# First attention of a two-layer gated cross-attention kernel: the last chunk's scores, the weighted sum of two steps back and the next step's first scores as one stretch of TensorE work

## The chip, the cores and the metric

The kernel runs on one core of a Trainium2 chip. The time is the device time of one execution in microseconds (us). The kernel before takes 2732.07 us, the median of three runs (2730.35, 2732.07, 2735.17).

## The reference, cut

Two layers follow each other. Each adds a gated cross-attention of 16 x 100 tokens of width 512 to a context of 16 x 722 rows of width 384, and then a gated feed-forward (in the first layer a mixture of 8 experts, in the second a quantized network). Everything is float32. The change touches the attention, above all that of layer 0:

```python
# layer 0: H = 16 heads, D = 32; layer 1: H = 8, D = 64, no biases on q, k, v
q = (layernorm(x) @ Wq + bq).reshape(B, Nq, H, D).transpose(0, 2, 1, 3)   # B=16, Nq=100
k = (ctx @ Wk + bk).reshape(B, Nkv, H, D).transpose(0, 2, 1, 3)           # Nkv=722
v = (ctx @ Wv + bv).reshape(B, Nkv, H, D).transpose(0, 2, 1, 3)
attn = softmax(clip(einsum('bhqd,bhkd->bhqk', q, k) * D**-0.5, -1e4, 1e4), axis=-1)
x = x + tanh(g_xattn[0]) * (einsum('bhqk,bhkd->bqhd', attn, v).reshape(B, Nq, C) @ Wo + bo)
```

## The kernel before, in words

The program runs layer 0's attention, the routing and the experts, layer 1's attention and the quantized network one after the other. Both attentions are objects of one class, `Attention`. A group holds G heads that fill 128 rows: G is 4 in the first attention (32 rows each) and 2 in the second (64 rows each). One **step** is a pair (b, m), batch b and group m; there are 16 x 4 = 64 steps in each attention.

In a step the keys lie on the 128 partitions, in NS = 6 chunks of the 722 context rows; the last chunk has SL = 82 rows. NS1 is 5. Queries (T = 100) and heads lie along the free dimension. The parts of a step are:

- `scores(b, m, 0)`, L362: the *first scores*, chunks 0 to 4. Twenty matmuls (L372), four heads at a time in 32-row tiles of the array, write one PSUM tile `ps_s`. In the first attention this tile takes four of the eight PSUM banks, and the pool has one buffer of it (`4 // self.G`, L261); in the second it has two. ScalarE copies the tile to the SBUF tile `raw` (L386). VectorE then takes maxima in two reductions (L389): over chunks 0 to 2, and over that result with chunks 3 and 4, into a tile `mx`.
- `scores(b, m, 1)`: the *last chunk's scores*, four matmuls into the same PSUM tile, a copy by ScalarE (L382) and one maximum into `mx` (L384).
- `peaks`, L393: TensorE transposes `mx` (L399), VectorE reduces the transposed maxima over the partitions (L405).
- `softmax`, L407: TensorE transposes the tops back and spreads them over 128 partitions (L413, `ps_top`). VectorE subtracts them from the scores in three instructions (L421: chunks 0 to 2, chunks 3 and 4, the last chunk), ScalarE takes two exponentials of 1200 elements a partition (L427), and GpSimd (VectorE in the second attention) adds the six chunks into `sm` (L430).
- `attend`, L435: the *weighted sum*. 24 matmuls (L442) in 32-column tiles form probabilities times values, four more (L453) the denominators from `sm`; VectorE divides (L461, L462).

Besides these there is full-size TensorE work, which I call *dense units*: `keys` (L216, three matmuls of 361 columns), `values` (L241, three of 512), `queries` (L345), `project` (L468), transposes of inputs (L139), and, for the experts that follow, normalized rows and their logits (L657). A float32 matmul that is not a transpose stands as two records in the trace, so a value chunk shows as six.

`run`, L496, writes out the order of TensorE's work. For each step it collects dense units with due times (`first`, `last`) and an even share of their cost. Then it issues, in this order: `peaks` of step i, first scores of step i+1, dense units of a cost of at least 2000 columns, `softmax` of step i, last chunk's scores of step i+1, weighted sum of step i-1, and the rest of the dense units. TensorE keeps that order (`manual_schedule(engines={PE})`). On the other engines a scheduler places the instructions, and each engine runs its own in that order. The dense units, `ps_mx`, `ps_top` and the weighted sum share a PSUM pool `ps_m` of four one-bank buffers.

SP's queue issues the context loads (`load_ctx`, two buffers); a batch's load is issued in the third step of the batch two before it.

Of the kernel before, what the change touches and what calls it, by code (L numbers as in the profile page):

```python
# [8 lines left out]
F32 = mybir.dt.float32  # L9
I32 = mybir.dt.int32  # L10
AF = mybir.ActivationFunctionType
ALU = mybir.AluOpType
AX = mybir.AxisListType
# [3 lines left out]
P = 128  # L17
B, T, C = 16, 100, 512
# [5 lines left out]
KC = C // P  # L24
KK = CK // P
NS = -(-S // P)
SL = S - (NS - 1) * P
NS1 = NS - 1
# [12 lines left out]
BIG = 3.0e38  # L41
# [9 lines left out]
def bcast(ap, *shape):  # L51
    return ap.to_broadcast(list(shape))
# [90 lines left out]
class Attention:  # L143
# [113 lines left out]
    def open(self, ctx):  # L257
        tc, nc, name, w = self.net.tc, self.net.nc, self.name, self.w
        pool = lambda n, k, **kw: open_pool(ctx, tc, f"{name}_{n}", k, **kw)
        self.pb, self.pw, self.p2 = pool("b", 1), pool("w", 1), pool("2", 2)  # L260
        self.ps_s, self.ps_m = pool("s", 4 // self.G, space=PSUM), pool("m", 4, space=PSUM)  # L261
        if not hasattr(self, "wq"):
            self.wq = self.pw.tile([P, KC, C], F32, name=f"wq_{name}")
        self.wo = self.pw.tile([P, KC, C], F32, name=f"wo_{name}")
        for n in ("bq", "bv"):
            if n + "_cols" in w:
                self.cols[n] = self.pw.tile([P, KC], F32, name=f"{n}c_{name}")
                nc.gpsimd.dma_start(self.cols[n], w[n + "_cols"])
        self.gbo = self.pw.tile([P, C], F32, name=f"gbo_{name}")

        self.tT = self.pw.tile([P, KC, N], F32, name=f"tT_{name}")

        self.raw = [
            self.pw.tile([P, self.G, NS + 1, T], F32, name=f"raw{i}_{name}") for i in range(2)
        ]
        for t in self.raw:
            nc.gpsimd.memset(t[:, :, NS, :], -BIG)
        self.qT, self.mx, self.top, self.pT = {}, {}, {}, {}

    def load_query_weights(self, pin=False):  # L280

# [80 lines left out]
    def scores(self, b, m, part):  # L362


        nc, D, G = self.net.nc, self.D, self.G
        g, i = divmod(b, GB)
        q = slice(i * T, (i + 1) * T)
        ps = self.ps_s.tile([P, G, 512], F32, tag="s", name="ps_s")
        r = SL if part else P
        for n, c in enumerate((NS - 1,) if part else range(NS - 1)):  # L370
            for j in range(G):
                nc.tensor.matmul(  # L372
                    ps[:r, j, n * T : (n + 1) * T],
                    self.kT[b, m][j * D : (j + 1) * D, c * P : c * P + r],
                    self.qT[g][j * D : (j + 1) * D, m, q],
                    start=True,
                    stop=True,
                )

        st = self.raw[(b * KC + m) % 2]  # L380
        if part:
            nc.scalar.copy(st[:SL, :, NS, :], ps[:SL, :, :T])  # L382
            mx = self.mx[b, m]
            nc.vector.tensor_tensor(mx, mx, st[:, :, NS, :], ALU.max)  # L384
            return
        nc.scalar.copy(st[:, :, :NS1, :].rearrange("p g c t -> p g (c t)"), ps[:, :, : NS1 * T])  # L386
        mx = self.mx[b, m] = self.p2.tile([P, G, T], F32, tag="mx", name="mx", bufs=1)
        for c, to in ((0, st[:, :, NS1, :]), (3, mx)):
            nc.vector.tensor_reduce(  # L389
                to, st[:, :, c : c + 3, :].rearrange("p g c t -> p g t c"), AX.X, ALU.max  # L390
            )

    def peaks(self, b, m):  # L393

        nc, G = self.net.nc, self.G
        mx = self.mx.pop((b, m))
        ps = self.ps_m.tile([T, G, P], F32, tag="mm", name="ps_mx")
        for j in range(G):
            nc.tensor.transpose(ps[:, j, :], mx[:, j, :], self.net.ident)  # L399
        if self.extremes is None:  # L400
            self.top[b, m] = self.p2.tile([T, G], F32, tag="top", name="top")
        else:
            h = b * self.heads + m * G
            self.top[b, m] = self.extremes[:, h : h + G]
        nc.vector.tensor_reduce(self.top[b, m], ps, AX.X, ALU.max)  # L405

    def softmax(self, b, m):  # L407

        nc, G = self.net.nc, self.G
        top, st = self.top.pop((b, m)), self.raw[(b * KC + m) % 2]  # L410
        ps = self.ps_m.tile([P, G, T], F32, tag="mm", name="ps_top")
        for j in range(G):
            nc.tensor.transpose(ps[:, j, :], bcast(top[:, j : j + 1], T, P), self.net.ident[:T, :T])  # L413
        t = self.p2.tile([P, 2, G, 3, T], F32, tag="pT", name="pT")

        late = b == B - 1 and m
        adds = nc.gpsimd if G == 4 else nc.vector
        sm = None if late else self.p2.tile([P, G, T], F32, tag="sm", name="sm")
        for part in range(2):
            for c, z, at in ((0, 3, 0),) if part == 0 else ((0, 2, 3), (2, 3, NS)):  # L420
                nc.vector.tensor_tensor(  # L421
                    t[:, part, :, c:z, :],
                    st[:, :, at : at + z - c, :],
                    bcast(ps.unsqueeze(2), P, G, z - c, T),
                    ALU.subtract,
                )
            nc.scalar.activation(t[:, part], t[:, part], AF.Exp)  # L427
            for n in () if late else range(3):
                if part or n:
                    adds.tensor_tensor(  # L430
                        sm, t[:, part, :, n, :], sm if part or n > 1 else t[:, 0, :, 0, :], ALU.add
                    )
        self.pT[b, m] = t, sm

    def attend(self, b, m):  # L435
        nc, D, G = self.net.nc, self.D, self.G
        t, sm = self.pT.pop((b, m))
        ps = self.ps_m.tile([P, 2, T], F32, tag="mm", name="ps_pv")
        for c in range(NS):
            n = P if c < NS - 1 else SL  # L440
            for j in range(G):
                nc.tensor.matmul(  # L442
                    ps[j * D : (j + 1) * D, 0, :],
                    self.v[b][:n, c, m * P + j * D : m * P + (j + 1) * D],
                    t[:n, c // 3, j, c % 3, :],
                    start=(c == 0),
                    stop=(c == NS - 1),
                )

        parts = [sm] if sm is not None else [t[:, c // 3, :, c % 3, :] for c in range(NS)]  # L450
        for k, of in enumerate(parts):
            for j in range(G):
                nc.tensor.matmul(  # L453
                    ps[j * D : (j + 1) * D, 1, :],
                    self.net.ones[:, :D],
                    of[:, j, :],
                    start=(k == 0),
                    stop=(k == len(parts) - 1),
                )
        rs = self.p2.tile([P, T], F32, tag="rs", name="rs")  # L460
        nc.vector.reciprocal(rs, ps[:, 1, :])  # L461
        nc.vector.tensor_tensor(self.tT[:, m, b * T : (b + 1) * T], ps[:, 0, :], rs, ALU.mult)  # L462
# [33 lines left out]
    def run(self, done=(), after_project=None, more=()):  # L496
# [14 lines left out]
        for b in range(B):  # L511
            for i in tiles_for(b):

                at = (b + 1) * KC + (1 if b != B - 2 else KC - 1)
                extra[at].append((self.project, i))
                for later, *unit in after_project(i) if after_project else ():
                    extra[at + later].append(tuple(unit))
        todo = [u for b in range(1, B) for u in self.keys_and_values(b) if u not in done]

        def do(units):  # L520
            for f, *a in units:
                f(*a)

        def first(unit):

            f, b, n = unit[:3]
            return 4 * (b - 1) + n - 1 if f == self.keys else 4 * (b - 1) if b > 1 else -1

        def last(unit):

            f, b, n = unit[:3]
            return 4 * b + n - 2 if f == self.keys else 4 * b

        end = len(steps) - 2
        for i in range(-1, len(steps)):
# [11 lines left out]
                    todo.remove(unit)  # L547
                    spent += self.cost(unit)

            units.sort(key=lambda u: u[0] in (self.keys, self.values) and first(u) == i)  # L550
            nxt = steps[i + 1] if i + 1 < len(steps) else None
            u = self.cut(units, 2000)
            if i >= 0:
                self.peaks(b, m)
            if nxt:
                self.scores(*nxt, 0)
            if self.G == 4:
                do(u[0])
                if i >= 0:
                    self.softmax(b, m)  # L560
            if nxt:
                self.scores(*nxt, 1)
            if i > 0:
                self.attend(*steps[i - 1])
            if self.G == 2:
                do(u[0])
                if i >= 0:
                    self.softmax(b, m)
            do(u[1])
        self.attend(*steps[-1])  # L570
        for i in range(len(steps), len(steps) + 40):
            do(extra[i])
# [1045 lines left out]
```

## Time and profile before

| what | value |
|---|---|
| median of three runs | 2732.07 us |
| the profiled execution, its own time | 2731.8 us |
| its span, first to last instruction | 2730.1 us |
| granted TensorE clock, mean over the span | 0.992 |
| first attention, first scores of step 1 to those of step 63 | 55.3 to 864.26 us |
| TensorE busy in that stretch | 799.5 of 809.0 us |
| VectorE, ScalarE, GpSimd busy in that stretch | 546.3, 415.0, 357.0 us |

The profile names an engine PE (TensorE's matmuls), PEld (its weight loads), DVE (VectorE), ACT (ScalarE), POOL (GpSimd) or SP. A row of the time line gives the start in the span, the busy time and the group of instructions; what stands in brackets is how long the engine was idle before and which instruction ended that. `L372 PE MATMUL ps_s<-qT_a,kT_a 32*128` is a matmul of line 372 with 32 rows and 128 columns of weights. The trace also has each instruction's own record, from which the spacings of matmuls are read. Matmul ends are modelled, so it is the starts that count.

### The profile page before, as it was taken

The page shows a single profiled execution, that of the slowest core. Times are in us where ns is not written, and L with a number is a line of the kernel's source. Part 1 is how long each engine was busy: PE and PEld are TensorE (multiplying, and loading weights), DVE is VectorE, ACT ScalarE, POOL GpSimd, SP SyncE. Part 2 cuts the span into 40 slices and gives each one's busy share as a digit, 9 for nine tenths or more (in the row PEclk, how much of TensorE's full clock was granted, in tenths as well). Part 3 has the DMA queues.
Part 4 walks back from the last instruction along what each step waited for, and adds up shares of the span by engine and source line. Part 5 has one row for each costly group of instructions (what it writes and reads, how often), then busy time and mean ns, then how long its engine had stood idle before and what let it go on. Part 6 is the DMA issues. An engine that isn't in the chain of part 4 may idle for free. (4 is left out here: it accounts for less than half of the span.)

```text
span 2730.1 us, 45777 instructions
## 1 busy us (share of the span) xinstructions
PE 2682.5 (98%) x19716; PEld 1740.7 (64%) x19716; DVE 1201.2 (44%) x2010; ACT 859.0 (31%) x1194; POOL 499.3 (18%) x497
## 2 busy tenths in 40 slices
PE   8999999999998999999999999999999999899999
PEld 5666666666565688888888766666666566445554
DVE  4666676666667301010101077666565555611100
ACT  2545554545454100000000046333333333311110
POOL 2534444444442000000000042000000000301000
PEclk9999999999999899999999999999999999999999
DMA  5001000010001499989899432000000010610000
GB/s 167 18 18 34 18 29 22 18 45 18 18 29 57 169 360 348 320 313 321 310 318 319 166 91 63 21 22 29 17 23 27 17 34 1 185 62 16 12 12 10
DMA packets 129190, 278.33 MB, mean 102 GB/s; under 512 B 5825, under 2 KB 5841, under 8 KB 128465
## 3 DMA queue, kind: packets, MB, share of 16 engines
q1 hardware_dynamic: 117888, 246.80, 26.2%
q0 software_dynamic: 5968, 19.17, 2.1%
q10 hardware_dynamic: 5120, 9.31, 0.9%
q8 instruction: 160, 2.62, 0.4%
q14 instruction: 54, 0.43, 0.0%
HBM read 260.31 MB, written 14.94 MB: 101 GB/s over the span
## 5 line engine op out<-in xcount | busy, mean ns | idle before, releaser
L241 PE MATMUL ps_v<-wv_a,ctx_a 128*128 128x512 f32 (+1 forms) x1152 | 520.2, 599 | 1.0 <-DVE pT L421 0.5
L216 PE MATMUL ps_k<-ctx_a,wk_a 128*128 128x361 f32 x1488 | 485.5, 473 | 3.2 <-DVE pT L421 2.1
L874 PE MATMUL ps_h<-xT,w 128*128 128x128 f32 x3712 | 422.1, 276 | 4.0 <-DVEq L1503 4.0
L874 PEld LDWEIGHTS ps_h<-xT,w 128*128 128x128 f32 x3712 | 419.5, 193 | 4.7 <-issue 4.7
L216 PEld LDWEIGHTS ps_k<-ctx_a,wk_a 128*128 128x128 f32 x1488 | 272.6, 190 | 164.0 <-issue 18.3
L241 PEld LDWEIGHTS ps_v<-wv_a,ctx_a 128*128 128x128 f32 (+1 forms) x1152 | 204.8, 184 | 243.1 <-issue 229.9
L427 ACT ACTIVATE pT<-pT 128x1200 f32<-128x1200 f32 (+1 forms) x256 | 243.2, 953 | 258.2 <-DVE pT L421 248.0
L421 DVE TENSOR_TENSOR pT<-raw_a,ps_top 128x400 f32<-128x400 f32 (+4 forms) x384 | 279.0, 771 | 11.2 <-PE ps_top L413 11.0
L430 POOL TENSOR_TENSOR sm<-pT,sm 128x400 f32<-128x400 f32 x244 | 252.5, 1035 | 38.4 <-ACT pT L427 21.7
L389 DVE TENSOR_REDUCE raw_a<-raw_a 128x400 f32<-128x1200 f32 (+1 forms) x128 | 152.1, 1188 | 218.0 <-ACT raw_a L386 217.9
L386 ACT COPY raw_a<-ps_s 128x2000 f32<-128x2000 f32 (+1 forms) x128 | 180.3, 1408 | 154.1 <-PE ps_s L372 153.7
L372 PE MATMUL ps_s<-qT_a,kT_a 32*128 32x100 f32 (+3 forms) x4608 | 214.2, 277 | 3.4 <-ACT raw_a L386 1.2
L885 DVE TENSOR_TENSOR midT<-silu,ps_h 128x512 f32<-128x512 f32 x58 | 39.9, 688 | 390.4 <-PE ps_h L874 390.4
L894 PE MATMUL ps_o<-w,midT 128*128 128x512 f32 x464 | 203.9, 592 | 0.0
L372 PEld LDWEIGHTS ps_s<-qT_a,kT_a 32*128 32x128 f32 (+3 forms) x4608 | 180.1, 180 | 35.8 <-issue 22.7
L1100 PE MATMUL ps_z<-ffn_w,y_ffn 128*128 128x512 f32 (+1 forms) x416 | 190.8, 594 | 0.0
L248 ACT COPY v_a<-ps_v 128x512 f32<-128x512 f32 x192 | 111.3, 581 | 248.3 <-PE ps_v L241 248.3
L1082 PE MATMUL ps_y<-hT,ffn_w 128*128 128x384 f32 (+2 forms) x512 | 183.6, 503 | 0.0
L442 PE MATMUL ps_pv<-pT,v_a 128*32 128x100 f32 (+3 forms) x4608 | 163.2, 254 | 7.3 <-ACT pT L427 7.3
L442 PEld LDWEIGHTS ps_pv<-pT,v_a 128*32 128x32 f32 (+3 forms) x4608 | 135.5, 120 | 22.6 <-ACT pT L427 8.7
L1082 PEld LDWEIGHTS ps_y<-hT,ffn_w 128*128 128x128 f32 x512 | 95.1, 190 | 84.6 <-issue 50.3
L894 PEld LDWEIGHTS ps_o<-w,midT 128*128 128x128 f32 x464 | 85.9, 190 | 97.1 <-issue 97.1
(169 smaller groups left out, 2211.3 us busy)
## 6 DMA issues: line engine op xcount, KB each, us to landing
w<-in_L_ffn_w SPq DMA_DIRECT2D x116, 1024.0 KB
w<-in_L_ffn_wo SPq DMA_DIRECT2D x29, 2048.0 KB
ctx_a<-in_ctxT SPq DMA_DIRECT2D x30, 1083.0 KB
q<-in_L_ffn_fc_q SPq DMA_DIRECT2D x8, 1024.0 KB
ffn_w<-in_L_ffn_fc_scales SPq DMA_DIRECT2D x8, 1024.0 KB
rows<-ot ACTq DMA_DIRECT2D x29, 256.0 KB
xn_d<-xn_moe POOLq DMA_DIRECT2D x11, 256.0 KB, 2.3
ctx_a<-in_ctxT SPq DMA_DIRECT2D x6, 361.0 KB
```

The lines of the kernel that those rows point to most:

```text
L216: nc.tensor.matmul(ps, self.wk[:, k, m * P : (m + 1) * P], self.cxs[b][:, k, c * SH : (c + 1) * SH], start=(k == 0), stop=(k == KK - 1),)
L241: nc.tensor.matmul(ps[:n], self.cxs[b][:, k, c * P : c * P + n], self.wv[:, k, :], start=(k == 0), stop=(k == KK - 1),)
L372: nc.tensor.matmul(ps[:r, j, n * T : (n + 1) * T], self.kT[b, m][j * D : (j + 1) * D, c * P : c * P + r], self.qT[g][j * D : (j + 1) * D, ...
L386: nc.scalar.copy(st[:, :, :NS1, :].rearrange("p g c t -> p g (c t)"), ps[:, :, : NS1 * T])
L421: nc.vector.tensor_tensor(t[:, part, :, c:z, :], st[:, :, at : at + z - c, :], bcast(ps.unsqueeze(2), P, G, z - c, T), ALU.subtract,)
L427: nc.scalar.activation(t[:, part], t[:, part], AF.Exp)
L430: adds.tensor_tensor(sm, t[:, part, :, n, :], sm if part or n > 1 else t[:, 0, :, 0, :], ALU.add)
L442: nc.tensor.matmul(ps[j * D : (j + 1) * D, 0, :], self.v[b][:n, c, m * P + j * D : m * P + (j + 1) * D], t[:n, c // 3, j, c % 3, :], start ...
L874: nc.tensor.matmul(ph[:, f, :], w[:, n, k, f * P : (f + 1) * P], self.xT[j][:, k, :], start=(k == 0), stop=(k == KC - 1),)
L894: nc.tensor.matmul(po, self.midT[j, f // 4][:, f % 4, :], w[:, f, :], start=(f == 0), stop=(f == KF - 1),)
L1082: nc.tensor.matmul(ps[:, :nt], w1[f // nf][:, k, f % nf * P : (f % nf + 1) * P], hT[g][:, k, :nt], start=(k == 0), stop=(k == KC - 1),)
L1100: nc.tensor.matmul(z[j][:n], y[:, j * P : j * P + n], w2[f // nf][:, f % nf, :], start=(f == 0), stop=(f == NF - 1),)
```

## The change

Seven edits, all in `Attention`:

1. In the first attention (G = 4) `run` issues, for step i: last chunk's scores of step i, weighted sum of step **i-2**, first scores of step i+1, dense units of at least 2500 columns, `peaks` of step i, dense units of at least 1500, `softmax` of step i, and the rest. At the end the weighted sums of the last two steps remain.
2. In the second attention the order of the calls stays as it was.
3. The due times of keys, values and projections move by one step in the first attention.
4. The tile `mx` goes. `raw` has seven chunks; now the last chunk's scores lie in place 5 and the maxima in place 6, behind them. Place 5 holds the maximum of chunks 0 to 2 until the last chunk's scores overwrite it.
5. The last chunk is treated on its 82 rows only (maximum, subtraction, exponential, addition, denominator), so the two memsets of `raw` go.
6. The softmax has three exponentials (1200, 800 and 400 elements in the first attention) in place of two of 1200, each behind its own subtraction, in both attentions.
7. Line numbers shift: in the changed kernel the matmuls of the scores are L370, the last chunk's copy L380, the maximum L382, the first scores' copy L384, the reductions L386, the subtractions L422, the exponentials L425, the additions L427, the weighted sum L439 and L451.

```diff
-        for t in self.raw:
-            nc.gpsimd.memset(t[:, :, NS, :], -BIG)
...
         if part:
-            nc.scalar.copy(st[:SL, :, NS, :], ps[:SL, :, :T])
-            mx = self.mx[b, m]
-            nc.vector.tensor_tensor(mx, mx, st[:, :, NS, :], ALU.max)
+            nc.scalar.copy(st[:SL, :, NS1, :], ps[:SL, :, :T])
+            mx = st[:SL, :, NS, :]
+            nc.vector.tensor_tensor(mx, mx, st[:SL, :, NS1, :], ALU.max)
             return
...
-        mx = self.mx[b, m] = self.p2.tile([P, G, T], F32, tag="mx", name="mx", bufs=1)
-        for c, to in ((0, st[:, :, NS1, :]), (3, mx)):
+        for c, to in ((0, NS1), (3, NS)):
...
-        for part in range(2):
-            for c, z, at in ((0, 3, 0),) if part == 0 else ((0, 2, 3), (2, 3, NS)):
-                nc.vector.tensor_tensor(
-                    t[:, part, :, c:z, :],
-                    st[:, :, at : at + z - c, :],
-                    bcast(ps.unsqueeze(2), P, G, z - c, T),
-                    ALU.subtract,
-                )
-            nc.scalar.activation(t[:, part], t[:, part], AF.Exp)
...
+        for a, z in ((0, 3), (3, NS - 1), (NS - 1, NS)):
+            r = P if z < NS else SL
+            to = t[:r, a // 3, :, a % 3 : a % 3 + z - a, :]
+            nc.vector.tensor_tensor(
+                to, st[:r, :, a:z, :], bcast(ps[:r].unsqueeze(2), r, G, z - a, T), ALU.subtract
+            )
+            nc.scalar.activation(to, to, AF.Exp)
...
-                at = (b + 1) * KC + (1 if b != B - 2 else KC - 1)
+                at = (b + 1) * KC + (KC - 1 if b == B - 2 else 2 if self.G == 4 else 1)
...
-            return 4 * (b - 1) + n - 1 if f == self.keys else 4 * (b - 1) if b > 1 else -1
+            lag = self.G == 4
+            at = 4 * (b - 1) + n - 1 if f == self.keys else 4 * (b - 1) if b > 1 else -2
+            return at + lag
...
-            return 4 * b + n - 2 if f == self.keys else 4 * b
+            return 4 * b + n - 2 if f == self.keys else 4 * b + (self.G == 4)
...
+            if self.G == 4:
+
+                if i >= 0:
+                    self.scores(b, m, 1)
+                if i > 1:
+                    self.attend(*steps[i - 2])
+                if nxt:
+                    self.scores(*nxt, 0)
+                one, units = self.cut(units, 2500)
+                do(one)
+                if i >= 0:
+                    self.peaks(b, m)
+                two, units = self.cut(units, 1500)
+                do(two)
+                if i >= 0:
+                    self.softmax(b, m)
+                do(units)
+                continue
...
-            if self.G == 4:
-                do(u[0])
-                if i >= 0:
-                    self.softmax(b, m)
-            if nxt:
                 self.scores(*nxt, 1)
             if i > 0:
                 self.attend(*steps[i - 1])
...
+        if self.G == 4:
+            self.attend(*steps[-2])
         self.attend(*steps[-1])
```

More of the change, by code (lines that the diff above doesn't have):

```diff
@@ L275, in open @@
         ]
-        for t in self.raw:
-            nc.gpsimd.memset(t[:, :, NS, :], -BIG)
-        self.qT, self.mx, self.top, self.pT = {}, {}, {}, {}
+        self.qT, self.top, self.pT = {}, {}, {}
     def load_query_weights(self, pin=False):
@@ L381, in scores @@
         if part:
-            nc.scalar.copy(st[:SL, :, NS, :], ps[:SL, :, :T])
-            mx = self.mx[b, m]
-            nc.vector.tensor_tensor(mx, mx, st[:, :, NS, :], ALU.max)
+            nc.scalar.copy(st[:SL, :, NS1, :], ps[:SL, :, :T])
+            mx = st[:SL, :, NS, :]
+            nc.vector.tensor_tensor(mx, mx, st[:SL, :, NS1, :], ALU.max)
             return
         nc.scalar.copy(st[:, :, :NS1, :].rearrange("p g c t -> p g (c t)"), ps[:, :, : NS1 * T])
-        mx = self.mx[b, m] = self.p2.tile([P, G, T], F32, tag="mx", name="mx", bufs=1)
-        for c, to in ((0, st[:, :, NS1, :]), (3, mx)):
+        for c, to in ((0, NS1), (3, NS)):
             nc.vector.tensor_reduce(
-                to, st[:, :, c : c + 3, :].rearrange("p g c t -> p g t c"), AX.X, ALU.max
+                st[:, :, to, :],
+                st[:, :, c : c + 3, :].rearrange("p g c t -> p g t c"),
+                AX.X,
+                ALU.max,
             )
@@ L395, in peaks @@
         nc, G = self.net.nc, self.G
-        mx = self.mx.pop((b, m))
+        mx = self.raw[(b * KC + m) % 2][:, :, NS, :]
         ps = self.ps_m.tile([T, G, P], F32, tag="mm", name="ps_mx")
@@ L418, in softmax @@
         sm = None if late else self.p2.tile([P, G, T], F32, tag="sm", name="sm")
-        for part in range(2):
-            for c, z, at in ((0, 3, 0),) if part == 0 else ((0, 2, 3), (2, 3, NS)):
-                nc.vector.tensor_tensor(
-                    t[:, part, :, c:z, :],
-                    st[:, :, at : at + z - c, :],
-                    bcast(ps.unsqueeze(2), P, G, z - c, T),
-                    ALU.subtract,
-                )
[L427 to L431, printed above, removed]
-                    )
+        for a, z in ((0, 3), (3, NS - 1), (NS - 1, NS)):
[5 more added lines that the diff above has]
+            nc.scalar.activation(to, to, AF.Exp)
+            for c in () if late else range(max(a, 1), z):
+                adds.tensor_tensor(
+                    sm[:r], t[:r, c // 3, :, c % 3, :], sm[:r] if c > 1 else t[:, 0, :, 0, :], ALU.add
+                )
         self.pT[b, m] = t, sm
@@ L451, in attend @@
         for k, of in enumerate(parts):
+            n = P if k < NS - 1 else SL
             for j in range(G):
@@ L454, in attend @@
                     ps[j * D : (j + 1) * D, 1, :],
-                    self.net.ones[:, :D],
-                    of[:, j, :],
+                    self.net.ones[:n, :D],
+                    of[:n, j, :],
                     start=(k == 0),
@@ L548, in run @@
                     spent += self.cost(unit)
-            units.sort(key=lambda u: u[0] in (self.keys, self.values) and first(u) == i)
+            if self.G == 2:
+                units.sort(key=lambda u: u[0] in (self.keys, self.values) and first(u) == i)
             nxt = steps[i + 1] if i + 1 < len(steps) else None
-            u = self.cut(units, 2000)
+            if self.G == 4:
[15 more added lines that the diff above has]
+                continue
+            one, units = self.cut(units, 2000)
             if i >= 0:
@@ L564, in run @@
                 self.attend(*steps[i - 1])
[L565 to L569, printed above, removed]
+            do(one)
+            if i >= 0:
+                self.softmax(b, m)
+            do(units)
+        if self.G == 4:
+            self.attend(*steps[-2])
         self.attend(*steps[-1])
```

## The prediction

> **What bounds the kernel now.** I read the page's busy times first, then TensorE's waits inside the first attention, then the time line of one of its steps, and last the two places where the same resource was short.
>
> The page: TensorE is busy for almost the whole span, the other engines are not.
> ```profile
> PE 2682.5 (98%) x19716; PEld 1740.7 (64%) x19716; DVE 1201.2 (44%) x2010; ACT 859.0 (31%) x1194; POOL 499.3 (18%) x497
> ```
> TensorE's waits between the first scores of step 1 (55.3 us) and of step 63 (864.26 us), 62 steps of 13.05 us (9.4 us in all by the idle time ahead of the groups):
> ```profile
> PE ps_mx L399 <- DVE mx L384: 3.4, 2, 2.1
> PE ps_k L216 <- DVE pT L421: 2.1, 2, 1.9
> PE ps_y L468 <- DVE pT L421: 1.9, 1, 1.9
> PE ps_mx L399 <- ACT pT L427: 1.2, 1, 1.2
> PE ps_v L241 <- DVE pT L421: 0.5, 2, 0.3
> ```
> The columns are total, times and longest. Nothing else stops TensorE there, so shorter TensorE work is worth its whole length, and a new wait costs its whole length.
>
> One step on the time line (start, busy us, engine, group):
> ```profile
> 300.92 0.51 PE L413 MATMUL ps_top<-ident,extremes 100*128 100x100 f32 x4
> 301.36 0.41 PE L372 MATMUL ps_s<-qT_a,kT_a 32*82 32x100 f32 x8
> 301.71 1.24 PE L442 MATMUL ps_pv<-pT,v_a 128*32 128x100 f32 x48
> 301.90 0.49 ACT L382 COPY raw_a<-ps_s 82x400 f32<-82x400 f32 x1 [0.19 <-PE ps_s L372]
> 302.77 0.36 PE L453 MATMUL ps_pv<-sm,ones 128*32 128x100 f32 x8
> 302.94 2.77 DVE L421 TENSOR_TENSOR pT<-raw_a,ps_top 128x1200 f32<-128x1200 f32 x3
> 303.05 5.42 PE L241 MATMUL ps_v<-wv_a,ctx_a 128*128 128x512 f32 x12
> 304.42 2.52 ACT L427 ACTIVATE pT<-pT 128x1200 f32<-128x1200 f32 x2 [2.03 <-DVE pT L421]
> 308.31 0.60 PE L399 MATMUL ps_mx<-ident,mx 128*100 128x128 f32 x4
> 308.84 1.37 PE L372 MATMUL ps_s<-qT_a,kT_a 32*128 32x100 f32 x40
> 310.14 0.66 PE L139 MATMUL ps_tr<-ident,xn_a 128*128 128x128 f32 x4
> 310.33 1.83 ACT L386 COPY raw_a<-ps_s 128x2000 f32<-128x2000 f32 x1 [1.24 <-PE ps_s L372]
> ```
> Two things are to be seen. The small-tile work (32-row and 32-column tiles) stands in two places. And ScalarE copies the last chunk's scores (301.90) ahead of the exponentials (304.42), over six microseconds before the next scores (308.84) need their PSUM tile.
>
> **The gain: one change of tile shape fewer.** Single records of the trace give the price. Before 308.84 the spacing is 0.202 us where two transposes stand 0.109 apart: 0.093 lost. After the weighted sum the first full-size matmul starts 0.177 later, and the second 0.533 instead of 0.429 after it: 0.281. The change removes both and adds one boundary, weighted sum to first scores, which no record shows. Bounds are 0.07 (groups inside the weighted sum) and 0.202. I take 0.177, since that spacing was the same before every kind of matmul. Saved: 0.093 + 0.281 - 0.177 = 0.197 us a step, 62 steps: **-12.2 us** (bounds -10.7 and -18.8). The boundary into the last chunk's scores costs 0.09 over the usual spacing before and after the change.
>
> **The new wait on ScalarE.** All scores of this attention go through one PSUM tile (four banks, one buffer). The next step's first scores now come 1.69 us (301.36 to 302.88, + 0.177) after the last chunk's, and must wait until ScalarE has copied those. In the changed program's instruction order ScalarE has, in nearly every step: copy of first scores, copies of the dense units before the top transposes, three exponentials, copies of the units after them, and only then the last chunk's copy. So exponentials that delayed nobody now stand ahead of a copy that TensorE waits for; behind that copy stand the next copy of scores and everything that follows it.
>
> Take a step whose three blocks of dense work are one value chunk each, time 0 at its first scores. TensorE: dense work at 1.303 (308.84 to 310.14), + 0.104 first matmul, value 2.58 (6 x 0.429), maxima's transposes 0.44, value 2.58: top transposes at 7.00. Then 0.35, value 2.58, 0.09, and 1.69 more: next first scores wanted at 11.71. The other chain: subtraction 0.62 after the top transposes begin (445.66 to 446.27): 7.62; exponential 1.48 later (302.94 to 304.42): 9.10; 1.21 for 1200 elements; then 800 and 400 elements, which this trace lacks. The rows of 1200 (1.203) and of 600 in the second attention (0.703) make a line with 0.20 fixed: 0.87 and 0.53. End 11.71; value copy 0.58; last chunk's copy 0.49; 0.06 to TensorE: 12.84. **Wait 1.13 us.** The same sum over all 62 steps, each with its own units in the changed order: 21 steps with one value behind the top, 1.13 each, 23.7; 22 with two key blocks, 0.61 to 0.90, 14.2; 3 with one key block, 1.9 each, 5.7; one with nothing, 3.8; the other 15, where more stands there, 1.6. Together **+49.0 us**. Bounds for the two shorter exponentials: 0.49 (copy of 400) + 0.70, and 0.70 + 1.20: -0.2 and +0.5 a step, -10 and +25 us on some 50 steps.
>
> **The wait at the top transposes.** VectorE's reduction of the transposed maxima (0.69) now stands behind the first, often behind both, reductions of the next step's scores (1.54 each), which begin at 1.49 + 1.83 + 0.04 = 3.36. With a query block ahead of the maxima and one key block behind: 3.36 + 1.54 + 0.62 (query) + 1.54 + 0.69 + 0.10 = 7.86, and TensorE comes at 6.36: 1.50. Such steps: 4 at 1.50, 9 at 0.86 (projection), 5 at 0.74, three more with 2.3 in all; 41 at nothing. **+19.7 us**; bounds 0 (were the reduction ahead) and 25.
>
> **What else goes and comes.** The old waits go, since their causes (maximum late behind the subtractions, a PSUM buffer held by them) now end before the row does: -9.4. Kept maxima: the maximum works on 82 partitions of the same 400 elements, 0.56, and the buffer it no longer shares was never waited for; the two memsets on GpSimd lie in the opening. GpSimd's five additions a step (1.03 each) have one step more to finish. The third exponential adds 0.20 to every step of the second attention, behind TensorE except in its few waits there: +0.5. Opening, one activation table load that falls into the chain, and the last step, where the projection moves ahead of the last maxima (877.69 - 874.45 = 3.2 us at most): 0.8 + 1.6 - 2.5. DMA issues on SP and GpSimd keep their steps; values may fall one step later, and the context load they free, 4.5 us long by the DMA share (issued 319.3, over by 323.8), still has a step of 13 us.
>
> **The clock.** A wait can cost more than itself:
> ```profile
> 595.95:599.37 3.42, 1.49 (x8) 0.94 (x7) 3.42 (x6) 2.36 (x2) 1.20 (x1) 1.00 0.00 0
> 599.37:602.78 3.41, 3.41 (x7) 1.88 (x6) 0.86 (x3) 0.61 (x2) 3.17 (x4) 0.50 0.02 5
> 836.50:840.00 3.50, 2.22 (x20) 1.00 (x22) 3.47 (x6) 1.96 (x3) 2.74 (x3) 1.00 0.00 0
> 840.00:843.40 3.40, 3.40 (x45) 2.05 (x39) 0.94 (x2) 1.82 (x1) 2.31 (x3) 1.00 0.02 5
> ```
> In the first column after the stretch's length TensorE is busy: 1.49 of 3.42 us was followed by a granted clock of 0.50 for 3.41 us, 2.22 of 3.50 was not. Half speed for 3.41 us loses 1.7. Four new waits of about 1.9 us or more, at rather better than half odds: +4 (bounds 0, and 1.7 for each of the 25 of 1.1 or more: 43).
>
> The Trainium skill, "TensorE: Matmul & The Clock Gate", section "Why this matters for your kernels", says that idle gaps up to about 3 us do not throttle. The trace differs: a gap of 1.9 us did. By the page this term would be 0 and the time 4 us less; the rows decide.
>
> **Sum**, against the profiled execution's own 2731.8 us (span 2730.1; 0.3 under the median 2732.07, nothing at this scale): -12.2 + 49.0 + 19.7 - 9.4 + 0.5 - 0.1 + 4 = +51.5, **2783 us**.
>
> **Rivals.** *Faster*: the last chunk's copy is never late. The row is then pure gain: -12.2 - 9.4 and the ends -2, with 0 to 19.7 for the reduction: 2708 to 2728. For it speaks that ScalarE is busy 31% only; against it the fixed order of its instructions, and that it happened in the one place where the tile is refilled at once:
> ```profile
> 865.76 1.82 ACT L386 COPY raw_a<-ps_s 128x2000 f32<-128x2000 f32 x1 [1.37 <-PE ps_s L372]
> 867.64 0.64 PE L372 MATMUL ps_s<-qT_a,kT_a 32*82 32x100 f32 x8 [1.15 <-ACT raw_a L386]
> ```
> It decides where both waits together stay under about 0.35 us a step (22 us). *Clock*: waits of 1.1 us also drop it: +43 in place of +4, 2822. *No gain from the row*: the new boundary costs as much as both old ones: +12, 2795, inside the range.
>
> **Chances.** Forecast 0.70, no gain from the row 0.05, clock 0.09, faster 0.12, waits and gain cancelling 0.04. The range reaches from 2783 - 10 (exponentials) - 7 (boundary) - 16 (most of the reduction's wait) to 2783 + 25 + 10: 2750 to 2818, which leaves out the faster rival and most of the clock's. This kernel's measurement tells 0.2% from no change: faster 0.13, same 0.03, slower 0.84.
>
> **What would show it.** TensorE's first scores (L370) waiting for the last chunk's copy (L380), about 49 us in some 50 waits; top transposes waiting for the reduction L405, about 20 us in 21; spacing 0.18 from weighted sum to first scores. It is wrong if the first scores follow the weighted sum without a wait, or if the exponentials are seen behind the last chunk's copy.

## The result and the profile after

| | before | after |
|---|---|---|
| median of the runs shown | 2732.07 us | **2748.11 us** (four runs, 2745.17 to 2751.44) |
| profiled execution, its own time | 2731.8 us | 2751.44 us |
| its span | 2730.1 us | 2749.4 us |
| first attention, first scores of step 1 to those of step 63 | 808.9 us | 821.6 us |

The ratio is 1.0058 with a 95% interval of 1.004 to 1.0075: the change costs 0.6%. The forecast was slower, 2783, with a range from 2750 to 2818. The direction was right; the size (+51.5 forecast, +16.0 measured) was three times too large, and the range missed the time by 2 us. The profiled execution of the changed kernel is the slowest of its four, 3.3 us above their median; what of that could be traced is told further down, under the remainder of the profiled execution.

The page of the changed kernel, the engines' busy times (us, share of the span, instructions) and the group of the scores (count, then busy us, mean ns, idle time ahead and what ended most of it):
```profile
PE 2682.1 (98%) x19716; PEld 1733.0 (63%) x19716; DVE 1209.9 (44%) x2010; ACT 855.2 (31%) x1322; POOL 503.1 (18%) x493
...
L370 PE MATMUL ps_s<-qT_a,kT_a 32*128 32x100 f32 (+3 forms) x4608 | 213.4, 277 | 20.9 <-ACT raw_a L380 18.8
```
TensorE's busy time is what it was (2682.5 before). The 19 us are idle time, and the second line names the forecast's wait: first scores behind the last chunk's copy. TensorE's waits in the loop, which reaches from 54.74 to 876.36 us here (view of 54 to 877 us; total, times, longest):
```profile
PE ps_s L370 <- ACT raw_a L380: 18.8, 27, 1.3
PE ps_top L413 <- DVE extremes L405: 11.3, 22, 1.0
PE ps_mx L399 <- DVE raw_a L382: 0.2, 1, 0.2
```
All the old waits but 0.2 us are gone and both new ones are there, at the lines the prediction named. Two of the 27 lie ahead of the first scores of steps 1 and 2, which have no weighted sum ahead of them. In the other 61 steps, by the starts of the matmuls (start to start, less the usual spacing of the same pair of lines), the waits are 18.6 us in 25 steps for the copy and 15.2 in 23 for the top transposes. Forecast were 49.0 in some 50 steps and 19.7 in 21.

One step of the changed kernel on its time line, all engines, with the rows of the chain alone (start, busy us, engine, group):
```profile
363.96 0.56 PE L413 MATMUL ps_top<-ident,extremes 100*128 100x100 f32 x4 [0.25 <-DVE extremes L405]
...
364.63 2.78 DVE L422 TENSOR_TENSOR pT<-raw_a,ps_top 128x1200 f32<-128x1200 f32 x3 [0.72 <-PE ps_top L413]
...
366.06 2.39 ACT L425 ACTIVATE pT<-pT 128x1200 f32<-128x1200 f32 x3 [1.73 <-DVE pT L422]
...
368.36 0.56 ACT L248 COPY v_a<-ps_v 128x512 f32<-128x512 f32 x1
...
368.83 0.49 ACT L380 COPY raw_a<-ps_s 82x400 f32<-82x400 f32 x1
...
369.37 0.37 PE L370 MATMUL ps_s<-qT_a,kT_a 32*128 32x100 f32 x4 [0.56 <-ACT raw_a L380]
```
The chain is the forecast's, link by link: top transposes, subtraction, three exponentials, value copy, last chunk's copy, first scores. But look at the starts on ScalarE. The three exponentials are busy 1.202, 0.854 and 0.521 us, 2.58 in sum, and the group lasts 2.39. It ends at 368.456, and the value copy has already begun at 368.362. Each instruction starts 0.093 to 0.097 before the one ahead of it has ended. From top transposes to first scores the chain takes 5.41 us; the prediction's links sum to 5.84.

### The profile page after: what moved, and what is told of

The parts are those of the page before. It is cut to its first block, busy times and chain, and to the rows that moved or that the text cites. A ratio compares the mean times of both kernels' runs of the same rounds, so it can differ in the third digit from the quotient of the medians.

```text
span 2749.4 us, 45695 instructions
## 1 busy us (share of the span) xinstructions
PE 2682.1 (98%) x19716; PEld 1733.0 (63%) x19716; DVE 1209.9 (44%) x2010; ACT 855.2 (31%) x1322; POOL 503.1 (18%) x493
## 5 line engine op out<-in xcount | busy, mean ns | idle before, releaser
L386 DVE TENSOR_REDUCE raw_a<-raw_a 128x400 f32<-128x1200 f32 (+1 forms) x256 | 298.5, 1166 | 184.4 <-ACT raw_a L384 183.4
L425 ACT ACTIVATE pT<-pT 128x1200 f32<-128x1200 f32 (+5 forms) x384 | 243.1, 693 | 174.0 <-DVE pT L422 167.5
L422 DVE TENSOR_TENSOR pT<-raw_a,ps_top 128x1200 f32<-128x1200 f32 (+5 forms) x384 | 276.5, 769 | 45.0 <-PE ps_top L413 43.4
L427 POOL TENSOR_TENSOR sm<-pT,sm 128x400 f32<-128x400 f32 x244 | 264.5, 1084 | 19.1
L370 PE MATMUL ps_s<-qT_a,kT_a 32*128 32x100 f32 (+3 forms) x4608 | 213.4, 277 | 20.9 <-ACT raw_a L380 18.8
L384 ACT COPY raw_a<-ps_s 128x2000 f32<-128x2000 f32 (+1 forms) x128 | 180.3, 1408 | 169.6 <-PE ps_s L370 169.6
L370 PEld LDWEIGHTS ps_s<-qT_a,kT_a 32*128 32x128 f32 (+3 forms) x4608 | 179.3, 180 | 84.3 <-issue 47.3
L439 PE MATMUL ps_pv<-pT,v_a 128*32 128x100 f32 (+3 forms) x4608 | 163.0, 254 | 6.7 <-ACT pT L425 6.7
L439 PEld LDWEIGHTS ps_pv<-pT,v_a 128*32 128x32 f32 (+3 forms) x4608 | 135.2, 120 | 22.0 <-ACT pT L425 8.0
```

Source lines behind the costliest of these rows:

```text
L370: nc.tensor.matmul(ps[:r, j, n * T : (n + 1) * T], self.kT[b, m][j * D : (j + 1) * D, c * P : c * P + r], self.qT[g][j * D : (j + 1) * D, ...
L386: nc.vector.tensor_reduce(st[:, :, to, :], st[:, :, c : c + 3, :].rearrange("p g c t -> p g t c"), AX.X, ALU.max,)
L422: nc.vector.tensor_tensor(to, st[:r, :, a:z, :], bcast(ps[:r].unsqueeze(2), r, G, z - a, T), ALU.subtract)
L425: nc.scalar.activation(to, to, AF.Exp)
L427: adds.tensor_tensor(sm[:r], t[:r, c // 3, :, c % 3, :], sm[:r] if c > 1 else t[:, 0, :, 0, :], ALU.add)
L439: nc.tensor.matmul(ps[j * D : (j + 1) * D, 0, :], self.v[b][:n, c, m * P + j * D : m * P + (j + 1) * D], t[:n, c // 3, j, c % 3, :], start ...
```

## The theory and its rivals, before the experiments

**Theory.** The row itself gains what was forecast. Two new waits take it back, each with its own cause: the copy L380 stands behind the exponentials on ScalarE, and the reduction L405 behind the reductions L386 on VectorE. The forecast was too high because the instructions of the ScalarE chain were added end to end although they overlap. **Rivals:** the third exponential and the kept maxima cost the time; the waits are not ScalarE's; the clock or the end of the first attention makes the loss.

## Experiments

The time of the kernel before in the runs beside e1 to e4 was 2732.16 us (median of 21), beside e5 to e8 2731.64 (of 9).

**e1_layout: the new data layout in the old order.** `run` is taken from the kernel before; the kept maxima, the 82-row last chunk and the three exponentials stay in both attentions.
```diff
-                if i > 1:
-                    self.attend(*steps[i - 2])
-                if nxt:
-                    self.scores(*nxt, 0)
-                one, units = self.cut(units, 2500)
...
+            u = self.cut(units, 2000)
+            if i >= 0:
+                self.peaks(b, m)
+            if nxt:
+                self.scores(*nxt, 0)
...
```


> The order of the kernel before with the new softmax and the maxima kept in the raw tile (three exponentials in both attentions, no memsets). Theory (the loss comes from the new order alone): the first attention's loop stays at 809 us, and the whole at the time before, 2732, plus 0 to 3 us for the third exponential in the second attention, where the stage is 3.1 us longer in the changed kernel's profile: 2731 to 2736. Rival (the three exponentials and the kept maxima cost the time): most of the 16 us, 2742 to 2748.

Measured: 2733.03 us, ratio 1.0005 (0.9996 to 1.0014). Waits of the loop, 55 to 864.3 us:
```profile
PE ps_mx L399 <- DVE raw_a L382: 4.1, 3, 2.1
PE ps_k L216 <- DVE pT L422: 2.2, 2, 1.9
PE ps_y L466 <- DVE pT L422: 1.9, 1, 1.9
PE ps_v L241 <- DVE pT L422: 0.5, 2, 0.3
```
These are the old waits of the kernel before, nearly to the tenth. The layout costs nothing that can be measured, and the second attention's stage (first scores to last scores) is 742.05 us, against 742.20 before and 745.31 in the changed kernel: its third exponential is hidden. So the whole loss is the order's, its due times included.

**e2_double_copy: the suspected copy made longer.**
```diff
-            nc.scalar.copy(st[:SL, :, NS1, :], ps[:SL, :, :T])
+            for _ in range(G // 2):
+                nc.scalar.copy(st[:SL, :, NS1, :], ps[:SL, :, :T])
```


> The changed kernel with the last chunk's copy on ScalarE (L380) done twice in the first attention. Theory (this copy's end behind the exponentials sets when TensorE may start the next step's first scores): the copy's end against the wanted start is read from the changed kernel's trace for each of 61 steps; with 0.39 to 0.45 us more on each, 47 to 50 steps wait in place of 25 and the sum of the waits rises by 18 to 21 us, from 18.6 to about 38: 2766 to 2769. Rival (ScalarE's chain is not what the first scores wait for, or has room): within 3 us of 2748.

Measured: 2776.95 us (1.0162, 1.0149 to 1.0176), +28.8 over the changed kernel where 18 to 21 were expected. Waits of the loop, 54 to 909 us:
```profile
PE ps_s L370 <- ACT raw_a L381: 44.9, 49, 1.9
PE ps_top L414 <- DVE extremes L406: 8.7, 20, 1.0
...
```
The wait answers to the copy's length, as only the theory has it: where the changed kernel has 27 such waits of 18.8 us, this one has 49 of 44.9. By starts the sum is 45.4 us over the 61 steps, 26.8 more than in the changed kernel; each late step waits 0.51 to 0.52 more, the expectation took 0.39 to 0.45. The records show why: the second copy, which writes the same place, starts 0.03 us after the end of the first in all 60 pairs that stand side by side in the loop, while other neighbours on ScalarE overlap. The rest fits the clock: in the changed kernel it never fell to half inside the loop; here it did in four periods of 3.41 us, each behind a wait of 1.80 to 1.96, and half of a period, 1.7 us, is lost in each. A fifth wait of 1.96, at 812.9 us, was not followed by one. In the profiled executions the loop is 31.3 us longer: 26.8 of this wait and 0.5 of the same wait in step 2, 6.8 of clock, and 2.8 less at the top transposes. The clock was not in the expectation.

**e3_late_exp: the exponentials out of the chain.** They are issued behind the next step's last chunk's copy and pinned there; the weighted sum that reads them is a step later still.
`all_exps` holds the three exponentials and the additions that `softmax` had; `EXPS` holds the three ranges of chunks, (0, 3), (3, NS - 1) and (NS - 1, NS).
```diff
                 if i >= 0:
                     self.scores(b, m, 1)
+                if i > 0:
+                    self.all_exps(*steps[i - 1], self.EXPS[0:])
...
-            nc.scalar.activation(to, to, AF.Exp)
...
+        ins = nc.scalar.activation(to, to, AF.Exp)
+        if G == 4:
+            self.net.tc.keep_in_program_order(ins)
```


> The changed kernel with the three exponentials of a step placed on ScalarE behind the next step's last chunk's copy (order on ScalarE: last chunk's copy, three exponentials, copy of first scores), where they lie beside the weighted sum of two steps back. Theory: the wait of the first scores for that copy goes, 18.6 us; the copy of the first scores comes up to 0.2 us later in some steps, and with it the waits at the top transposes grow by up to 3 us: 2729 to 2733, no more than the kernel before. Rival (another engine is late next: the additions on GpSimd or the copy of the first scores): 2740 or more. Rival (clock and the end of the first attention make the loss): 2744 to 2748.

Measured: 2734.90 us (1.0009, 1.0000 to 1.0018), 13.2 less than the changed kernel where 15 to 19 were expected. Waits, 53 to 864 us:
```profile
PE ps_top L415 <- DVE extremes L405: 18.9, 24, 2.4
PE ps_s L370 <- ACT raw_a L380: 1.3, 2, 0.7
```
The first wait is gone in all 61 steps that have a weighted sum ahead of their first scores (the two that are left lie in the first two steps). The second grew by 7.7 us by starts (15.2 to 22.9), more than the 3 expected. Its longest, 2.4 us, has a link I had not counted; ScalarE and VectorE ahead of it:
```profile
557.18 0.48 ACT L380 COPY raw_a<-ps_s 82x400 f32<-82x400 f32 x1
557.68 1.28 ACT L435 ACT_TABLE_LOAD   x1
...
558.97 2.39 ACT L435 ACTIVATE pT<-pT 128x1200 f32<-128x1200 f32 x3
...
561.27 1.80 ACT L384 COPY raw_a<-ps_s 128x2000 f32<-128x2000 f32 x1
...
563.10 1.53 DVE L386 TENSOR_REDUCE raw_a<-raw_a 128x400 f32<-128x1200 f32 x1 [3.58 <-ACT raw_a L384]
```
An activation table load of 1.28 us stands ahead of the exponentials in the few steps that follow a square root of the layer normalisation. Here the copy of the first scores, and VectorE's reductions with it, start behind that. Four steps of the loop have such a load; there the copy starts 2.96 to 3.56 us after the first scores begin, against 1.5 in the changed kernel, and these steps account for 5.4 of the 7.7 us. At 834.1 us another 1.9 come from work for the experts' routing that VectorE does ahead of the reductions.

**e4_late_exp_top_first: both waits taken away.** e3, with VectorE's two reductions of the next scores issued behind `peaks` and the first of them pinned there.
```diff
                 if i >= 0:
                     self.peaks(b, m)
+                if nxt:
+                    self.maxima(*nxt)
```


> The kernel e3 with, besides, VectorE's two reductions of the next step's scores placed behind the reduction of the transposed maxima (L405). Theory: the waits of the top transposes go too, 15 us; subtractions end later by 1 to 2 us, which nobody waits for now: 2713 to 2720, faster than both kernels. Rival (the reductions and subtractions now late delay the next step's maximum or the exponentials): 2730 or more.

Measured: **2711.78 us**, ratio 0.9923 (0.9909 to 0.9936), faster than both kernels and 1.2 us below the expectation's lower end. Waits, 53 to 841 us:
```profile
PE ps_s L370 <- ACT raw_a L380: 1.8, 3, 0.7
PE ps_top L423 <- DVE extremes L413: 1.3, 1, 1.3
```
TensorE's order is that of the changed kernel, so the two loops can be set against each other matmul by matmul. This one takes 787.65 us against 821.62, 34.0 less: 18.6 ahead of the first scores (0.6 of it in step 2), 13.7 ahead of the top transposes, 1.3 as wider spacings among and just behind the top transposes, 0.4 ahead of the maxima's transposes, and under 0.1 elsewhere.

**e5_tail: the due time of the last projections.** e4, with the last sample's projections one step earlier.
```diff
-                at = (b + 1) * KC + (KC - 1 if b == B - 2 else 2 if self.G == 4 else 1)
+                at = (b + 1) * KC + (KC - 1 if b == B - 2 else 2 if self.G == 4 and b < B - 1 else 1)
```


> The kernel e4 with the last sample's two projections one step earlier, ahead of the two tiles' logits as in the kernel before. Theory (the changed due time of these projections costs the end of the first attention 3 to 5 us: the last weighted sum to the last projection took 15.1 us in the changed kernel, in e3 and in e4, 10.2 in the kernel before and 12.2 in e1): that stretch falls to 10 to 12.5 us, the whole to 2707 to 2709. Rival (the stretch is longer because the granted clock drops there whatever the order): it stays at 15 and the whole within 1.5 us of 2711.8.

Measured: **2708.89 us**, ratio 0.9917 (0.9903 to 0.9930); the best of this study. The end of the first attention on TensorE, first in the changed kernel, then in e5:
```profile
897.63 0.66 PE L139 MATMUL ps_tr<-ident,xn_moe 128*128 128x128 f32 x4 [1.46 <-POOL xn_moe L124]
899.07 1.81 PE L672 MATMUL ps_logits<-wg_sb,xnT_moe 128*128 128x8 f32 x8 [0.78 <-DVE xnT_moe L140]
900.74 9.87 PE L466 MATMUL ps_y<-wo_a,tT_a 128*128 128x512 f32 x16
```
```profile
860.90 0.66 PE L139 MATMUL ps_tr<-ident,xn_moe 128*128 128x128 f32 x4 [1.46 <-POOL xn_moe L124]
861.39 7.18 PE L489 MATMUL ps_y<-wo_a,tT_a 128*128 128x512 f32 x16
```
The 16 matmuls of the projections take 9.87 us in the one and 7.18 in the other. In the changed kernel the logits come first, wait 0.78 us more, and the clock is at half from 899.17 for 6.83 us. With the projections ahead it does not fall here. Last weighted sum to last projection is 9.8 us, 15.1 in the changed kernel. But the order does not settle the clock by itself. In e2, which has the logits ahead, the clock does not fall there and the stretch takes 11.7 us, so the order alone costs about 1.5 over the 10.2 of the kernel before, and the half clock 3.4. It fell there in five of the six profiled executions with the logits ahead, and in one of the four with the projections ahead (e1, for 3.41 us). The rival is therefore only partly out.

**e6_top_first_alone: one wait's remedy without the other's.** The diff of e4, without that of e3.

> The changed kernel with VectorE's reductions of the next step's scores behind the reduction of the transposed maxima (L405), the exponentials left where the change has them. Theory (the exponentials stand in the chain to the first scores, so whatever delays the subtractions delays TensorE): the waits of the top transposes go (-15 us), but the subtractions start behind both reductions and the wait for the last chunk's copy grows from 18.8 to about 83 us by the sum over the steps of e4's and the changed kernel's records: about +49, 2797, and 2800 to 2815 if some ten waits of 2 us or more drop the clock. Rival (the two waits add, each with its own remedy): 2748 - 15 = 2733.

Measured: 2781.49 us (1.0185, 1.0170 to 1.0201). Waits, 53 to 912 us:
```profile
PE ps_s L370 <- ACT raw_a L380: 58.7, 51, 3.3
...
```
The wait at the top transposes is gone, and the kernel is 33 us slower than the changed one: the two waits do not simply add. While the exponentials stand in the chain, VectorE's reductions ahead of the subtractions make it longer. My number was too high: by starts the wait is 59.1 us in the 61 steps, where about 83 were expected. The records show one reason: since the subtractions come later, ScalarE's order has one copy of a dense unit fewer between the exponentials and the last chunk's copy in 38 of 64 steps, about 0.5 us each.

**e7_triple_copy: what a wait costs beyond itself.** e2 with three copies.

> The changed kernel with the last chunk's copy done three times. Theory: the sum of the waits for it rises from e2's 43.5 us to 67 to 73, so 2800 to 2807 by the waits alone. In e2 the clock fell to half for 3.41 us in four places, all at waits of about 1.9 us. Now 5 waits are longer than 1.9 us and some 20 lie at 1.55 to 1.65: if only the former drop the clock, 2800 to 2815; if the latter do too, at 1.7 us each, 2835 or more.

Measured: 2834.10 us (1.0368, 1.0352 to 1.0383). The waits sum to 79.1 us by starts in the 61 steps, more than the 67 to 73 expected. The loop is 82.3 us longer than in the changed kernel: 60.5 of this wait and 1.0 of the same wait in step 2, some 25 of clock (15 half-clock periods in the loop, which ends at 958.2 us, 1.7 us each), and 3.7 less at the top transposes. The time is near the upper expectation, but not in the way it had it. In these steps, 20 waits of 1.59 to 1.71 us were followed by a half clock in only 4 places, and 8 waits of 1.89 to 3.03 in all 8. Two waits, of 1.67 and of 1.69 us, in stretches of 3.41 us (bounds, length, busy of PE, PEld, DVE, ACT, POOL with counts, granted clock, DMA share, GB/s):
```profile
152.24:155.65 3.41, 2.02 (x42) 1.69 (x43) 1.45 (x3) 1.85 (x4) 3.17 (x4) 1.00 0.02 5
155.65:159.06 3.41, 3.41 (x14) 1.93 (x13) 2.13 (x3) 1.25 (x1) 0.60 (x1) 1.00 0.00 0
165.90:169.31 3.41, 1.79 (x46) 1.56 (x43) 1.60 (x3) 1.85 (x5) 3.17 (x4) 1.00 0.02 5
169.31:172.72 3.41, 3.41 (x7) 1.91 (x6) 1.84 (x2) 1.77 (x2) 0.85 (x1) 0.50 0.00 0
```
The stretches are cut on the grid on which every half-speed period of this execution begins. The first wait starts at 151.96 and has 1.38 us in its stretch; the second starts at 165.85 and has 1.64. The clock falls behind the second and not behind the first. A longer wait shows the same: 2.3 us ahead of the first scores of step 2, at 68.1 us, is cut in two by the grid (TensorE busy 2.28 and 2.22 us in the two stretches), and the clock did not fall.

**e8_exp_behind_first_copy.** e5, with the exponentials behind the copy of the first scores too.

> The kernel e5 with the three exponentials behind the copy of the next first scores too (order on ScalarE: last chunk's copy, first scores' copy, exponentials). Theory: the copy of the first scores no longer stands behind an activation table load of 1.28 us (in e3 it started 1.4 us late in the one step that had one there); VectorE starts no sooner in the other steps: within 2 us of e5, 0 to 2 us faster. Rival (the copies of the dense units, now behind the exponentials, hold PSUM buffers that TensorE needs): 5 us or more slower than e5.

Measured: 2713.18 us (0.9930, 0.9917 to 0.9944), 4.3 slower than e5: neither side. Waits, 53 to 846 us:
```profile
PE ps_pv L474 <- POOL sm L447: 2.1, 1, 2.1
...
```
One weighted sum, at 114.4 us, waited 2.1 us for the additions on GpSimd, which follow the exponentials and begin there at 108.83 only; a half-clock period began behind that wait, at 115.1. Another, at 849.0, lies in the last steps. The loop of the profiled execution is 2.9 us longer than e5's and the last steps after it 1.8, so these two places make most of the loss. No wait of the rival's kind, for a PSUM buffer of a dense unit, appears. So the slack is small: with the exponentials one copy later, the additions are the next thing late.

## Why the prediction was right in direction and wrong in size

- **Bound, boundary, old waits: right.** Weighted sum to first scores is 0.177 us in the median, as taken. In e4, without the new waits, the loop less what is left of waits is 785.3 us, against 798.8 before; 1.7 of that is a half-clock period that the changed kernel and e4 do not have. That leaves about -11.8, forecast -12.2. The old waits are gone, -9.4.
- **The failed step: "The new wait on ScalarE", 49.0 us, measured 18.6.** Mechanism, place and order were right, and e2, e3 and e4 show them; the size of the chain was not. The prediction put 1.21, 0.87, 0.53, 0.58 and 0.49 us one behind the other. The durations were right within 0.02, but at each of the four joints the next instruction starts about 0.094 early: 0.38 of the 0.43 us. With small errors in the other links every step came out about half a microsecond too late. Where 1.13 was forecast, 0.63 was measured; 1.9 became 1.35; and the steps with two key blocks, forecast at 0.61 to 0.90, just do not wait (in 21 steps the copy ends at most 0.05 us ahead of the need). Half a microsecond in the 46 steps that wait, or just do not wait, is 23 of the missing 30 us. The stated bounds of -10 and +25 were bounds of the durations only; the joint was not among them. It could have been read: in the kernel before, the value copy of the quoted step starts at 306.85, and the second exponential ends at 306.94. Of its loop's pairs of ScalarE instructions, 89 overlap, by 0.093 in the median. The Trainium skill, "ScalarE: Activation LUTs", section "What ACT_TABLE_LOAD costs", has it too: "Back-to-back ACTIVATEs overlap by ≈ 93 ns." The trace agrees: 0.094 us between exponentials, and 0.094 to 0.102 in the median for pairs with a copy. It does not hold everywhere: the doubled copies of e2, which write the same place, do not overlap.
- **The wait at the top transposes: 19.7 forecast, 15.2 measured**, in 23 steps for 21. Inside its bounds.
- **Clock: +4 forecast, none in the loop.** The longest wait is 1.35 us there, not 3.8, so waits of the size that the term counted did not occur. Where they did occur, in e2, e6 and e7, clock was lost behind most of them.
- **Third exponential: +0.5 forecast, nothing found** (e1).
- **The ends: -0.1 forecast, about +4 measured** (opening -0.6, last step -0.3, last weighted sum to last projection +5.0). The 5.0 come with the changed due time of the projections: about 1.5 are the order itself, 3.4 the half clock that fell there (see e5). e5 takes 5.3 back in that stretch, 2.9 in the medians. I had counted the step's own projection and overlooked the logits that now come ahead of the last two. That the time came within 2 us of the range is in part luck: these 4 us, which were not forecast, made up for some of what the first wait lacked.
- **The remainder of the profiled execution.** Its second attention's stage is 3.1 us longer than that of the kernel before, with the same instructions in the same order as in e1. Over the profiled runs that stage lies between 742.05 and 745.67. These stretches show one cause; the same two waits of TensorE (0.9 and 1.2 us) lie in them, in the changed kernel and in e1:
```profile
1656.93:1660.34 3.41, 1.28 (x24) 0.89 (x20) 1.76 (x3) 3.26 (x6) 2.04 (x2) 1.00 0.09 34
1660.34:1663.75 3.41, 3.41 (x12) 2.38 (x13) 2.76 (x5) 0.00 (x0) 0.00 (x0) 0.50 0.00 0
```
```profile
1637.05:1640.46 3.41, 2.70 (x40) 2.04 (x38) 1.39 (x5) 3.35 (x5) 1.51 (x3) 1.00 0.77 309
1640.46:1643.87 3.41, 1.99 (x22) 1.56 (x23) 2.58 (x5) 2.02 (x5) 1.01 (x1) 1.00 0.00 1
1643.87:1647.28 3.41, 3.41 (x15) 2.10 (x13) 3.33 (x7) 0.68 (x2) 0.92 (x1) 1.00 0.00 0
```
In the changed kernel both waits fell into one stretch of the grid (1.28 us busy), and the next ran at half clock. In e1 the grid's edge parted them (2.70 and 1.99 busy), and nothing happened. The four executions with such a period at this place (changed kernel, e3, e4, e7) take 745.22 to 745.67 us for the stage, the six without it 742.05 to 744.35. Of the 3.3 us more than in e1, matmul by matmul, 1.6 arise at the half clock and 1.7 in the first 30 us of the stage. The cause of the latter is open; e8 loses 2.0 there too, without the period.
- **Open.** The loop of the changed kernel is accounted for by its two waits and the wider spacings behind them (see e4). Not tried was a change of the joint itself: that the overlap on ScalarE is what the sum lacked is read from the records of the changed kernel, not from a run that takes it away.

## What to carry to other kernels

A chain of instructions on one engine is summed from starts, not from busy times: read a pair of neighbours of each kind in the trace and subtract the overlap at every joint that has one, since an error of half a microsecond decides whether a step waits at all. When a step is pipelined more deeply, give the slack to the work that has it: here the exponentials had a whole step to spare and yet stood ahead of the one copy that TensorE waited for, and moving them, together with two reductions on VectorE, turned +0.6% into -0.8% with the same order on TensorE (e4). Moving them alone gave +0.1% (e3). Two waits in series are removed together or in the order of the chain, for e6 took away the shorter and made the longer more than three times as long.

## What the runs showed of the hardware

- In each execution all half-speed periods begin on one grid of 3.413 us, whose phase differs from run to run. In the ten profiled executions, from the first scores of step 1 to the last projection of the first attention, all 19 stretches of the grid in which TensorE was busy less than 1.6 of 3.41 us were followed by one, and 13 of the 35 stretches between 1.6 and 2.0. Of some 2400 above 2.0 it was 19: in 16 the half speed of the stretch itself went on, and three (2.42, 2.47 and 2.58 us busy, in e2 and e7) show that the busy time of one stretch is not the whole rule. A wait of 1.7 us thus costs 1.7 or 3.4, by where it falls (e7), and the same instructions can differ by some us between executions (742.05 to 745.67 for the second attention's stage). The Trainium skill, "TensorE: Matmul & The Clock Gate", section "What's actually happening", names a window of 3413 ns that does not start with the kernel; the traces agree.
- Successive ScalarE instructions overlap by 0.093 us in the median of the 89 pairs that do (kernel before); two copies that write the same place do not, the second starts 0.03 us after the first's end (e2, e7). An activation table load takes 1.28 us (e3) and stands in whatever chain its user stands in.
